# Instructions placed anew in a fused two-layer attention kernel: L0's fours, an attention transfer, odd norms, output weights, a copy and the last store

## The chip, the cores and the metric

The kernel runs on one core of a Trainium2 chip. The metric is the device time of one execution in microseconds (us), the median of several runs. The core has five engines with a queue of instructions each: the tensor engine (PE, with its weight loads shown apart as PEld), the vector engine (DVE), the scalar engine (ACT), GpSimd (POOL) and the sync engine (SP), which here only issues DMAs. POOL and ACT issue DMAs too. Each engine takes its instructions in the order in which they were written; a semaphore makes one wait for another engine.

## The reference

Two layers run one after the other on x and c (`ctx_1024`), both 32 batches of 256 tokens with 256 features in float32.

```python
# L0: 16 heads of 16 features; only batch 0 of the attention is used
q, k, v = x @ Wq.T, c @ Wk.T, c @ Wv.T           # split into heads
att = softmax(q k^T / 4) v
x = x + att[0]                                   # the same 256x256 block for all 32 batches

# L1: one head, a small hidden layer (4 wide), then a second attention
nX = layernorm(c, norm1)                         # keys and values
nF = layernorm(x, norm2)                         # queries
a  = softmax(nF nX^T / 16) nX
h  = gelu(a @ fc1_w.T + fc1_b)                   # 256 -> 4
ca = h @ fc2_w.T + fc2_b                         # 4 -> 256
n  = layernorm(ca, norm3)
s  = softmax(n n^T / 16) n
out = nF + gamma2 * (ca + gamma1 * s)
```

## The kernel before

**Layout.** Of a batch, partition p holds tokens 2p and 2p+1, so a tile is 128 x 2 x 256; the first of the two rows is called even and the second odd. `x_all` keeps all of x in SBUF, in place from the load to the output. c comes in fours of batches (`cq`). The order of instructions is written out by hand (`tc.manual_schedule()`): the order of the Python calls is the order in each engine's queue.

**L0 (the head, to about 35 us).** Only batch 0 is attended. The 16 heads go in four groups of four, j = 0 to 3, called "fours". For each: `head_queries(j)` makes the scores sq with queries as rows (eight products, L445); `head_maxima` takes their row maxima on DVE (L486) into `m_all`; `head_less(j)` transposes these maxima (pm) and returns an addition on DVE that folds them into `qmT` (L498); `head_keys(j)` makes the scores sk with keys as rows and their exponentials on ACT (L507); `head_values(j)` sums the values (ph, L357) and copies them to `col_h`; `head_turned(j)` transposes this (pt_h) and returns the division on DVE (L527, L528) that writes a quarter of `att`. The scores use six PSUM banks in turn; ph, pt_h, pm, pp_v, p_b1f share two banks of the tag "tp", and a tile that takes a bank waits for the last reader of the one before it. Between these stand small preparations: `project_values(1)` (pp_v), `setup_bias` (p_b1f, and `fc1b_all` on DVE), and `stats(n)`, the statistics of c's batch n (two DVE instructions, L211), from which `moments_c` makes the factors of the layernorm on POOL (the power at L227 is the long one), and `even_normed` (POOL) and `odd_normed` (ACT) apply them. `moments_ahead(2)` does its first part on DVE.

**att to x.** x0 to x3 get att by additions on DVE (`add_first`, L828). For the other batches `add_attention(lo, hi)` issues on POOL's queue a DMA that adds att to four batches of x_all (L751): seven transfers of 1 MB.

**L1's first attention.** `first_step(s)` runs for s = 0 to 34, one batch a step, in a software pipeline: in step s the scores of batch s are made (`cross_scores`, L779), their maxima taken on DVE (nm, L789) and their exponentials on ACT (e, L792). In the same step e of batch s-2 is transposed (`cross_turned`, pt_e) and copied by ACT to eTq (L801); x of batch s+1 is transposed (`turn_x`, pt_x) and scaled by ACT into nfT (L761); c of batch s+4 is transposed (`turn_c`, pt_c) and copied by DVE into nxT. `norm_x(n)` applies the layernorm to x: the even row on POOL (L329), the odd row on ACT (L331), up to four steps ahead of use. In every fourth step `moments_both` makes the factors of four batches of x and c on POOL. pt_x and pt_c alternate in the two "tp" banks, so that pt_x takes the bank of the last pt_c, and the other way round. Tables by step, `between` (before the scores) and `beside` (after the step), place the rest: `hide` and `activate` (the Gelu), `third_a` to `third_d` (the third layernorm and its products, w_k on POOL at L1010, t_k on DVE at L1055), `early_scores` and `early_weights` (the first pieces of the second attention), and the output weights: `output_gammas` (two products of 5 x 256 on DVE), `output_bias` (two), and `output_rows` (two, then eight small DMAs on SP that write w_out). In steps 27, 29 and 31 `cross_turned(s-2)` comes after the exponentials.

**L1's second attention.** From about 175 us a written list of words gives the order. "q", "k" and "o" are products, "max", "exp" and "sums" belong to the softmax, "scale" multiplies x by norm2's weight on POOL (L770), "add" adds two batches of output to x_all on DVE (L1214) and stores them with one DMA on SP (L1215).

Of the kernel before, what the change touches and what calls it, by code (L numbers as in the profile page):

```python
# [22 lines left out]
QB = 4  # L23
# [4 lines left out]
def tile_xattn_seq(  # L28
# [33 lines left out]
    nc = tc.nc  # L62
# [261 lines left out]
            )  # L324

    def norm_x(n, even=nc.gpsimd):
        rs, nmr, i = mx_of.pop(n)
        row = x_all[:, n, 0, :]
        even.tensor_scalar(row, row, rs[:, i, :], nmr[:, i, :], ALU.mult, ALU.add)  # L329
        row = x_all[:, n, 1, :]  # L330
        nc.scalar.activation(  # L331
            row, row, AF.Identity, bias=nmr[:, i + 1, :], scale=rs[:, i + 1, :]
        )
# [93 lines left out]
    def project_values(t, copy):  # L427
        pp = bank("tp", f"pp_v{t}")
        for dc in range(NC):
            nc.tensor.matmul(  # L430
                pp[:, t, :],
                c0T[:, dc, t * P : (t + 1) * P],
                wvT[:, dc, :],
                start=(dc == 0),
                stop=(dc == NC - 1),
            )
        copy(v1[:, t, :, 0:DK], pp[:, t, :].rearrange("p (h e) -> p h e", e=DK))
# [39 lines left out]
    def head_queries(j):  # L477

        sq = four_banks(f"sq{j}")
        qk = qT[:, j, :], kT[:, j, :]  # L480
        pair_products((0, *qk, sq[0:2]), (1, *qk, sq[2:4]))
        return sq

    def head_maxima(j, sq, heads):
        for i in heads:
            nc.vector.tensor_reduce(  # L486
                m_all[:, j % 2, :, i, ones_at[j % 2]], sq[i], AX.X, ALU.max, negate=True
            )
# [11 lines left out]
    def head_keys(j):  # L500

        sk = four_banks(f"sk{j}")
        kq = kT[:, j, :], qmT[:, j % 2, :]
        pair_products((0, *kq, sk[0:2]), (1, *kq, sk[2:4]))
        eT_of[j] = wk.tile([P, QB, NC, D], F32, tag="eTq", name=f"eT_h{j}", bufs=2)
        for i in range(QB):
            nc.scalar.activation(eT_of[j][:, i], sk[i], AF.Exp)  # L507
# [68 lines left out]
    def setup_bias():  # L576
        pb = bank("tp", "p_b1f")
        for dc in range(NC):
            nc.tensor.matmul(
                pb[:, 0, 0:FH], ones, b1f[:, dc, :], start=(dc == 0), stop=(dc == NC - 1)  # L580
            )
        nc.vector.tensor_add(fc1b_all, pb[:, 0, 0:FH], fc1b_bc)
# [82 lines left out]
    def stats(*ns):  # L665
        for n in ns:
            stats_c(n)
# [22 lines left out]
    head_less(1)()  # L690
    setup_outer()
    stats(3)
    project_values(1, on_scalar)
    moments_c(0)
    even_normed(0, 1, 2, 3)
    sq = head_queries(2)
    stats(4)
    head_maxima(2, sq, (0, 1))
    head_values(0)
    setup_bias()  # L700
    head_maxima(2, sq, (2, 3))
    head_keys(1)
    odd_normed(0, 1)
    weighted = head_turned(0)
    stats(5)
    head_less(2)()
    weighted()
    sq = head_queries(3)
    stats(6)
    head_maxima(3, sq, range(QB))  # L710
    head_values(1)
    odd_normed(2, 3)
    head_keys(2)
    weighted = head_turned(1)
    stats(7)
    moments_c(1)
    even_normed(4, 5)
    head_less(3)()
    weighted()
    head_keys(3)  # L720
    stats(8, 9, 10)
    head_values(2, by_vector)
    stats(11)
    odd_normed(4)
    head_values(3, on_scalar, True)
    c_ends = moments_ahead(2)
    weighted = head_turned(2), head_turned(3)
    for f in weighted:
# [21 lines left out]
    def add_attention(lo, hi):  # L750
        nc.gpsimd.dma_start(  # L751
            x_all[:, lo:hi],
            att.unsqueeze(1).to_broadcast([P, hi - lo, NC, D]),
            accum_op=ALU.add,
        )
# [38 lines left out]

        return softmax

    def cross_turned(n):
        q, b = n // QB, n % QB
        if b == 0:
            eT_of[q] = wk.tile([P, QB, NC, D], F32, tag="eTq", name=f"eTq_{q}", bufs=2)  # L800
        nc.scalar.copy(eT_of[q][:, b], turned(e_of.pop(n), "et", f"e_{n}"))  # L801

    def values(q):

# [64 lines left out]
    def first_step(s, between=()):  # L869
        q, b = s // QB, s % QB  # L870
        if b == 0 and 2 <= q and q + 4 < NQ:
            load_c(q + 4)
            if q == 2:
                load_x((NQ - 2) * QB, B)
        if s in (2, QB):
            add_attention((s // 2 + 2) * QB, (s // 2 + 3) * QB)
        elif b == 0 and 1 < q < NQ - 3:
            add_attention((q + 3) * QB, (q + 4) * QB)

        late_turn = s in (27, 29, 31)  # L880
        if 0 <= s - 2 < B and not late_turn:
            cross_turned(s - 2)
        if 2 <= s < 2 * QB:
            for n in (2 * s, 2 * s + 1):
                stats_x(n)
            if s < QB:
                ends = first_moments(2 * s, 2 * s + 2)
        if QB <= s and s + 3 * QB < B:
            stats_c(s + 3 * QB)
        if s >= 2 * QB and s + 2 * QB < B:  # L890
            stats_x(s + 2 * QB)
        if b == QB - 1 and 4 <= q + 2 < NQ:
            if q + 3 < NQ:
                moments_both(q + 2)
            else:
                moments_x(q + 2, 0, QB)
        if QB < s < B - 1:
            turn_x(s + 1)
        for n in {9: (12,), 10: (13, 14), 11: (15,)}.get(s, ()):
            norm_x(n)  # L900
        if 3 * QB <= s < B - 2 * QB:
            norm_x(s + QB)
        elif B - 2 * QB < s <= B - QB:
            norm_x(s + QB - 1)
        if s + QB < B and s >= QB:
            turn_c(s + QB, on_scalar if s < QB + 2 else by_vector)
        for n in {7: (13,), 8: (14, 15), 9: (16, 17), 10: (18,)}.get(s, ()):
            norm_c(n)
        if 2 * QB + 2 < s < B - 2 * QB:
            norm_c(s + 2 * QB)  # L910
        for n, at in enumerate(scaled_at):
            if s == at:
                scale_skip(n)
        if 2 * QB <= s < 2 * QB + len(zeroed):
            nc.gpsimd.memset(*zeroed[s - 2 * QB])
        if b == 2 and 1 < q < NQ:
            values_turned(q)
        if b == 1 and 1 < q < NQ:
            values(q)
        if b == 2 and 0 < q <= NQ:  # L920
            cross_values(q - 1)
        if b == 3 and 0 < q <= NQ:
            cross_weighted(q - 1)
        for f, *args in between:
            f(*args)
        if s < B:
            softmax = cross_scores(s)
            if s <= QB:
                turn_x(s + 1)
            if s == 0:  # L930
                turn_c(6, nc.scalar.copy)
            softmax()
        if late_turn:
            cross_turned(s - 2)
        if 1 <= s <= QB:
            stats_c(s + 3 * QB - 1)
        if s == 0:
            first_ends.pop()()
            add_first(3)
            first_ends.append(first_moments(3, QB))  # L940
            odd_normed(7)
        elif s == 1:
            first_ends.pop()()
            odd_normed(8)
            even_normed(8, 9)
        elif s == 2:
            ends()
            turn_c(7)
            load_c(5)
            odd_normed(9)  # L950
            even_normed(10)
        elif s == 3:
            ends()
            values(1)
            even_normed(11)
        elif s == QB:
            values_turned(1)
        if s in (QB, QB + 1):
            odd_normed(s + 6)
        if s == QB:  # L960
            moments_x(2, 0, 2)
        elif s == QB + 1:
            norm_x(2 * QB)
            moments_x(2, 2, QB)
        elif s == QB + 2:
            norm_x(2 * QB + 1)
            moments_c(3)
            norm_x(2 * QB + 2)
            norm_c(3 * QB)
        elif s == QB + 3:  # L970
            norm_x(2 * QB + 3)
        elif s == 2 * QB:
            moments_both(3)
# [179 lines left out]
    def activate(lo):  # L1153
# [1 line left out]

    between = {
        20: [(hide, 0, 4)],
        24: [(output_gammas,)],
        25: [(output_bias,)],
        27: [(output_rows,)],  # L1160
        28: [(turn_t, 0, by_vector)],
        29: [(turn_u, 2, by_vector), (early_weights, 0), (hide, 4, 6)],
        30: [(activate, 4), (third_a, 2), (turn_t, 1, by_vector)],
# [3 lines left out]
        20: [(activate, 0), (third_a, 0)],  # L1167
        21: [(third_b, 0), (third_a, 1)],
        22: [(third_c, 0), (third_b, 1)],
        24: [(third_d, 0)],  # L1170
        25: [(third_c, 1), (turn_u, 0, by_vector)],
        26: [(turn_u, 1, by_vector), (early_scores, 0), (third_d, 1)],
        28: [(early_scores, 1)],
# [37 lines left out]
    def output(p, pieces):  # L1211
# [2 lines left out]
            nc.vector.tensor_add(xs, po, xs)  # L1214
        nc.sync.dma_start(by_tokens(out[2 * p : 2 * p + 2]), x_all[:, 2 * p : 2 * p + 2])  # L1215


    held = {}

# [35 lines left out]
    turn_t6 add8 scale27 sums7 tT6 add7 turn_v5 col7 scale28 o9@s1+k12@s0 vT5 k13@et  # L1255
    add9 exp12 scale29 turn_a7 exp13 o10@s0+o11@s1 scale30 a7 sums6 add10 scale31
    turn_v7 col6 add11 vT7 turn_a6 o15@s0+o14@et a6 turn_v6 add15 vT6 o12@s1 add14
    o13@s0 add12 add13
    """

    def turn_a(g):
# [15 lines left out]
    def pre(lo):  # L1277
# [9 lines left out]
        "max": lambda p: scores_max(p, held.pop(("q", p))),  # L1287
        "exp": lambda p: weights(p, held.pop(("k", p))),
        "add": lambda p: output(p, held.pop(("o", p))),
        "a": lambda g: divide(g, held.pop(("a", g))),  # L1290
        "sums": sums,
        "col": col,
# [69 lines left out]
```

## Time and profile before

| | us |
|---|---|
| median of three runs | 227.26 (227.24 to 228.19) |
| the profiled execution: time | 228.16 |
| its span, first to last instruction | 226.4 |
| PE busy | 208.1 (92% of the span) |
| POOL busy | 175.3 (77%) |
| DVE busy | 169.8 (75%) |
| ACT busy | 146.6 (65%) |
| granted TensorE clock, mean | 0.992 |

The durations in this document come from the one profiled execution, whose time is 0.9 us above the median and whose span leaves 1.8 us around it. A row of the timeline gives start, length, engine, line, operation, output<-input, shapes, the count of equal instructions in the row, and in brackets the idle time before it with the one that ended it. Lengths of instructions that follow each other overlap a little, since an engine starts one before the last has left it: what an instruction costs its queue is the distance between starts.

### The profile page before, as it was taken

What the parts mean: (1) busy time and instruction counts of PE and PEld (TensorE: products, weight loads), DVE (VectorE), ACT (ScalarE), POOL (GpSimd) and SP (SyncE); (2) the same over time, 40 slices, a digit from 0 to 9 for tenths busy, and PEclk for the clock granted to TensorE, in tenths of its full rate; (3) what the DMA queues carried; (4) which work ended last, traced back from release to release, by engine and by line L of the source; (5) the groups of instructions that cost most, each with busy time, mean ns of one, the idle gap of its engine ahead of it and who ended that gap; (6) DMA issues with size and microseconds to landing.
All of it is one profiled execution on the core that took longest, in us unless ns stands there. A gap on an engine that the chain in (4) does not pass through costs nothing.

```text
span 226.4 us, 4951 instructions
## 1 busy us (share of the span) xinstructions
PE 208.1 (92%) x1797; PEld 152.6 (67%) x1797; DVE 169.8 (75%) x406; ACT 146.6 (65%) x301; POOL 175.3 (77%) x276
## 2 busy tenths in 40 slices
PE   7899988898999989999999999998998999999960
PEld 6666547576787859688798697685756566666640
DVE  2787989898988766768767578596546699978791
ACT  2454877698979359576868986448594684545510
POOL 6056588567889999999979989999229888999700
PEclk9999999999999999999999999999999999999996
DMA  6699998998976994082280000000000031542786
GB/s 210 214 310 375 389 386 225 179 263 246 208 145 244 305 195 185 0 147 43 48 142 0 1 3 0 0 3 5 5 1 0 3 126 62 210 164 92 278 308 254
DMA packets 18038, 33.81 MB, mean 149 GB/s; under 512 B 1175, under 2 KB 2142, under 8 KB 18014
## 3 DMA queue, kind: packets, MB, share of 16 engines
q1 hardware_dynamic: 12974, 24.33, 30.1%
q0 software_dynamic: 3696, 7.34, 18.6%
q10 hardware_dynamic: 1344, 1.84, 2.5%
q8 instruction: 14, 0.23, 0.4%
q14 instruction: 10, 0.08, 0.1%
HBM read 17.73 MB, written 8.39 MB: 115 GB/s over the span
## 4 chain that ended last, share of the span: by engine, by line
PE 45%; POOL 22%; DVE 14%; DMA 8%; ACT 5%; issue 3%; DVEq 1%; ACTq 0%; SPq 0%; POOLq 0%
PE sc L779 8%; POOL cq L307 6%; PE o L445 4%; DMA x_all<-att 4%; POOL rs_b L227 4%; PE k L445 4%; DVE st L211 4%; PE pu L357 4%; POOL x_all L329 3%; PE sc L445 2%; PE q L445 2%; DVE nm L789 2%; DMA wk_nat<-in_L_xattn_Wk_dram 2%; DMA fc_nat<-in_L_xattn_fc_w_dram 2%; POOL rs_x L227 2%
## 5 line engine op out<-in xcount | busy, mean ns | idle before, releaser
L779 PE MATMUL sc<-nxT,nfT 128*128 128x256 f32 x256 | 62.4, 386 | 0.7 <-ACT nfT L761 0.7
L779 PEld LDWEIGHTS sc<-nxT,nfT 128*128 128x128 f32 x256 | 45.7, 190 | 12.1 <-issue 5.3
L770 POOL TENSOR_TENSOR x_all<-x_all,w_bc 128x512 f32<-128x512 f32 x32 | 39.8, 1278 | 0.0
L792 ACT ACTIVATE e<-sc,nm 128x256 f32<-128x256 f32 x64 | 26.9, 474 | 19.2 <-DVE nm L789 19.0
L789 DVE TENSOR_REDUCE nm<-sc 128x2 f32<-128x512 f32 x32 | 22.0, 688 | 22.3 <-PE sc L779 10.7
L761 ACT ACTIVATE nfT<-pt_x,bq,wq 128x256 f32<-128x256 f32 x64 | 33.3, 583 | 1.6 <-PE pt_x L202 1.5
L211 DVE BATCH_NORM_STATS2 st<-x_all 128x6 f32<-128x256 f32 x64 | 23.2, 412 | 1.5 <-DMA x_all<-att 1.4
L202 PE MATMUL pt_x<-ident,x_all 128*128 128x128 f32 x132 | 20.4, 276 | 1.5 <-POOL x_all L329 1.3
L202 PE MATMUL pt_c<-ident,cq 128*128 128x128 f32 x132 | 19.7, 276 | 1.9 <-ACT nfT L761 1.4
L1214 DVE TENSOR_TENSOR x_all<-o,x_all 128x1024 f32<-128x1024 f32 (+1 forms) x20 | 19.3, 1005 | 2.9 <-PE o L445 2.4
L202 PE MATMUL pt_e<-ident,e 128*128 128x128 f32 x128 | 19.5, 275 | 1.3 <-ACT eTq L801 0.7
L211 DVE BATCH_NORM_STATS2 st<-cq 128x6 f32<-128x256 f32 x56 | 20.6, 412 | 0.0
L1209 ACT ACTIVATE eT<-k 128x512 f32<-128x512 f32 (+1 forms) x19 | 14.3, 798 | 9.1 <-PE k L445 7.8
L307 POOL TENSOR_SCALAR cq<-cq,rs_b,nmr_b 128x256 f32<-128x256 f32 x32 | 19.4, 679 | 0.0
L202 PEld LDWEIGHTS pt_e<-ident,e 128*128 128x128 f32 x128 | 15.4, 141 | 5.0 <-ACT e L792 1.6
L801 ACT COPY eTq<-pt_e 128x512 f32<-128x512 f32 x32 | 18.4, 588 | 0.3 <-PE pt_e L202 0.3
L202 PEld LDWEIGHTS pt_x<-ident,x_all 128*128 128x128 f32 x132 | 15.2, 141 | 4.6 <-POOL x_all L329 2.4
L202 PEld LDWEIGHTS pt_c<-ident,cq 128*128 128x128 f32 x132 | 15.0, 141 | 3.6 <-ACT nfT L761 2.4
L345 DVE COPY nxT<-pt_c 128x512 f32<-128x512 f32 x23 | 15.6, 677 | 2.4 <-PE pt_c L202 2.4
L331 ACT ACTIVATE x_all<-x_all,nmr_b,rs_b 128x256 f32<-128x256 f32 x16 | 9.8, 619 | 11.0 <-POOL nmr_b L236 11.0
L445 PE MATMUL o<-w_out,vt 32*128 32x256 f32 x128 | 13.3, 400 | 0.6 <-ACT vt L1088 0.5
L445 PE MATMUL k<-tt,ut 32*128 32x256 f32 x112 | 13.6, 397 | 0.0
(222 smaller groups left out, 435.6 us busy)
## 6 DMA issues: line engine op xcount, KB each, us to landing
out_dram<-x_all SPq DMA_DIRECT2D x16, 512.0 KB
x_all<-att POOLq DMA_DIRECT2D x7, 1024.0 KB, 9.8
cq<-in_ctx_dram SPq DMA_DIRECT2D x6, 1024.0 KB
x_all<-in_x_dram SPq DMA_DIRECT2D x4, 1024.0 KB
x_all<-in_x_dram SPq DMA_DIRECT2D x1, 2048.0 KB
x_all<-in_x_dram SPq DMA_DIRECT2D x1, 1792.0 KB
cq<-in_ctx_dram ACTq DMA_DIRECT2D x1, 1024.0 KB
cq<-in_ctx_dram SPq DMA_DIRECT2D x1, 768.0 KB
```

Of the source, the lines that this page charges most:

```text
L202: nc.tensor.transpose(pt[:, dc, t * P : (t + 1) * P], src[:, t, dc * P : (dc + 1) * P], ident)
L211: nc.vector.bn_stats(st[:, t, :], src[:, t, :])
L307: nc.gpsimd.tensor_scalar(row, row, rs[:, i + t, :], nmr[:, i + t, :], ALU.mult, ALU.add)
L345: copy(nxT_of[q][:, b], pt)
L445: nc.tensor.matmul(dst[i][:, t, :], lhs[r : r + SL, t * P : (t + 1) * P], rhs[r : r + SL, :], start=True, stop=True,)
L761: nc.scalar.activation(nfT_of[n][:, dc, :], px[:, dc, :], AF.Identity, bias=bq[:, dc : dc + 1], scale=wq2[:, dc : dc + 1],)
L770: nc.gpsimd.tensor_mul(x_all[:, n], x_all[:, n], w2_bc.unsqueeze(1).to_broadcast([P, NC, D]))
L779: nc.tensor.matmul(sc[:, qt, :], nfT[:, dc, qt * P : (qt + 1) * P], nxT[:, dc, :], start=(dc == 0), stop=(dc == NC - 1),)
L789: nc.vector.tensor_reduce(nm, sc, AX.X, ALU.max, negate=True)
L792: nc.scalar.activation(e[:, qt, :], sc[:, qt, :], AF.Exp, bias=nm[:, qt : qt + 1])
L801: nc.scalar.copy(eT_of[q][:, b], turned(e_of.pop(n), "et", f"e_{n}"))
L1214: nc.vector.tensor_add(xs, po, xs)
```

## The change

No computation is added or left out. Six things are placed anew:

1. In L0 the third four's maxima come at once, followed by the second four's keys; statistics of c's batches 4 to 7 and `setup_bias` stand at other places; the first two divisions come later; `head_values(2)` copies by ACT and not by DVE; the fourth four's values come before the statistics of batch 11.
2. `add_attention(12, 16)` is issued in step 0, behind the even row of x2, and not at the start of step 2.
3. `norm_x` is taken apart. The even rows stay; the odd rows of x12, x14, x16, x17 and x20 (x12 from step 9 to 10, x14 from 10 to 11, x16 from 12 to 13, x20 from 16 to 17) go with the next one.
4. `output_gammas` and `output_bias` go from before the scores of steps 24 and 25 to the end of step 23, `output_rows` from before the scores of step 27 to the end of step 24.
5. In step 31 e29's copy to eTq is DVE's and not ACT's.
6. The last pair of outputs is added and stored batch by batch.

```diff
@@ norm_x @@
     def norm_x(n, even=nc.gpsimd):
-        rs, nmr, i = mx_of.pop(n)
+        even_x(n, even)
+        odd_x(n)
+
+    def even_x(n, even=nc.gpsimd):
+        rs, nmr, i = mx_of[n]
         row = x_all[:, n, 0, :]
         even.tensor_scalar(row, row, rs[:, i, :], nmr[:, i, :], ALU.mult, ALU.add)
+
+    def odd_x(n):
+        rs, nmr, i = mx_of.pop(n)
         row = x_all[:, n, 1, :]
         nc.scalar.activation(
@@ L0 @@
     stats(3)
+    sq = head_queries(2)
+    stats(4)
     project_values(1, on_scalar)
     moments_c(0)
     even_normed(0, 1, 2, 3)
-    sq = head_queries(2)
-    stats(4)
-    head_maxima(2, sq, (0, 1))
+    head_maxima(2, sq, range(QB))
+    head_keys(1)
+    head_less(2)()
     head_values(0)
-    setup_bias()
-    head_maxima(2, sq, (2, 3))
-    head_keys(1)
+    stats(5, 6)
+    sq = head_queries(3)
     odd_normed(0, 1)
     weighted = head_turned(0)
-    stats(5)
-    head_less(2)()
-    weighted()
-    sq = head_queries(3)
-    stats(6)
     head_maxima(3, sq, range(QB))
     head_values(1)
     odd_normed(2, 3)
     head_keys(2)
-    weighted = head_turned(1)
+    setup_bias()
+    head_less(3)()
     stats(7)
     moments_c(1)
     even_normed(4, 5)
-    head_less(3)()
     weighted()
     head_keys(3)
+    weighted = head_turned(1)
+    weighted()
+    head_values(2)
     stats(8, 9, 10)
-    head_values(2, by_vector)
+    head_values(3, on_scalar, True)
     stats(11)
     odd_normed(4)
-    head_values(3, on_scalar, True)
     c_ends = moments_ahead(2)
@@ cross_turned @@
-    def cross_turned(n):
+    def cross_turned(n, copy=nc.scalar.copy):
...
-        nc.scalar.copy(eT_of[q][:, b], turned(e_of.pop(n), "et", f"e_{n}"))
+        copy(eT_of[q][:, b], turned(e_of.pop(n), "et", f"e_{n}"))
@@ first_step @@
-        if s in (2, QB):
-            add_attention((s // 2 + 2) * QB, (s // 2 + 3) * QB)
+        if s == QB:
+            add_attention(QB * QB, (QB + 1) * QB)
...
         for n in {9: (12,), 10: (13, 14), 11: (15,)}.get(s, ()):
-            norm_x(n)
+            even_x(n)
         if 3 * QB <= s < B - 2 * QB:
-            norm_x(s + QB)
-        elif B - 2 * QB < s <= B - QB:
+            even_x(s + QB)
+
+        for n in {10: (12, 13), 11: (14, 15), 12: (), 13: (16, 17), 16: (), 17: (20, 21)}.get(
+            s, (s + QB,) if 3 * QB <= s < B - 2 * QB else ()
+        ):
+            odd_x(n)
+        if B - 2 * QB < s <= B - QB:
             norm_x(s + QB - 1)
...
         if late_turn:
-            cross_turned(s - 2)
+            cross_turned(s - 2, by_vector if s == B - 1 else on_scalar)
...
         if s == 0:
             first_ends.pop()()
+            add_attention(3 * QB, 4 * QB)
             add_first(3)
@@ between, beside @@
         20: [(hide, 0, 4)],
-        24: [(output_gammas,)],
-        25: [(output_bias,)],
-        27: [(output_rows,)],
         28: [(turn_t, 0, by_vector)],
...
         22: [(third_c, 0), (third_b, 1)],
-        24: [(third_d, 0)],
+        23: [(output_gammas,), (output_bias,)],
+        24: [(third_d, 0), (output_rows,)],
         25: [(third_c, 1), (turn_u, 0, by_vector)],
@@ output @@
+    def output_each(p, pieces):
+
+        (_, _, po), = pieces
+        for n in range(2):
+            xs = x_all[:, 2 * p + n]
+            nc.vector.tensor_add(xs, po[:, n], xs)
+            nc.sync.dma_start(by_tokens(out[2 * p + n : 2 * p + n + 1]), x_all[:, 2 * p + n : 2 * p + n + 1])
...
-    o13@s0 add12 add13
+    o13@s0 add12 each13
...
+        "each": lambda p: output_each(p, held.pop(("o", p))),
```

## The prediction

> **What bounds the kernel now.** I read the chain of waits first, then the timeline of each engine at the places the diff touches, then busy time by stage. The page gives the tensor engine 92% of the span, so a place matters only if the tensor engine loses time there, or if a chain of other engines sets when it may go on. The chain of waits between 62 and 130 us (start, length, what) shows such a chain:
>
> ```profile
> 108.77 1.10 POOL cq L307 x2
> ...
> 109.96 9.85 DMA x_all<-att
> ...
> 119.90 0.75 DVE st L211 x2
> ...
> 126.71 0.66 PE pt_c L202 x4
> ```
>
> From 57 us to 115 us GpSimd runs without a gap (its timeline shows no idle there). The last attention transfer stands in that run at 109.96, lands 9.85 later, holds the vector engine's statistics of x28 to 119.90, and through maximum, exponential, Gelu and nfT it reaches a tensor engine that has waited 0.39 at 126.71. So whatever is gained between 57 and 126 counts only if GpSimd's run starts earlier. That start is a vector-engine chain. In the head (timeline of the vector engine; the bracket is the idle time before the row and who ended it):
>
> ```profile
> 20.31 1.29 DVE L486 TENSOR_REDUCE m_all<-sq 128x2 f32<-128x512 f32 x2 [0.97 <-PE sq L445]
> 21.87 0.16 DVE L582 TENSOR_TENSOR fc1b_all<-p_b1f,fc1b_bc 128x4 f32<-128x4 f32 x1 [0.27 <-PE p_b1f L579]
> ...
> 23.14 0.74 DVE L211 BATCH_NORM_STATS2 st<-cq 128x6 f32<-128x256 f32 x2
> 23.88 0.42 DVE L498 TENSOR_TENSOR qmT<-pm,qT 128x256 f32<-128x256 f32 x1
> ...
> 33.74 0.21 DVE L527 RECIPROCAL rd_h<-pt_h 128x8 f32<-128x8 f32 x1 [0.61 <-PE pt_h L375]
> ...
> 34.84 0.69 DVE L828 TENSOR_TENSOR x_all<-x_all,att 128x512 f32<-128x512 f32 x1
> ```
>
> The vector engine has few gaps up to 34.84, where L0 ends, and two more (0.54, 0.51) up to 56.7. After 126.7 the tensor engine is nearly gapless (0.28 at 142.6, 0.87 at 155.05, 0.67 at 174.35). The end is a stream of stores: the DMA engines are full (share 0.98 to 1.06) from 219 to 224.5.
>
> **1. L0's order.** No work is added; col_h2 (0.33 between starts) moves from vector to scalar engine. I walk from qmT of the second four (17.61, unchanged). Spacings from the rows: maximum 0.60, one statistic 0.33, last maximum to qmT 0.65 to 0.73 (two transposes between), score product to first maximum 1.16, p_b1f to fc1b_all 0.65.
> - Statistics of c3, c4 to 19.27; the products sq2 now run before pp_v1, so the four maxima follow at once: 19.27 to 21.69. qmT2 22.41 (1.5 earlier than before), with 0.72 idle, since stats(5), which covered it, now stands behind; c5's and c6's statistics and the next maxima are queued behind that wait.
> - Statistics c5, c6 to 24.07. On the tensor engine pm 22.25, ph0 23.25, sq3: first maximum 24.41 (idle 0.34), last to 26.83. Before: 27.70.
> - But pt_h0, ph1, sk2 and p_b1f fill the tensor engine to 27.37, and pm3 takes p_b1f's bank, so it waits for fc1b_all (27.48; idle 0.65). qmT3 28.24 (idle 0.66), only 0.2 earlier.
> - c7's statistics, att0, a wait for pt_h1 behind sk3 (0.59), att1, then eight statistics (2.63), five moments (0.75): rd_h2 at 34.2, where before it was at 33.74.
> The idle sum goes from 2.2 to 2.96, work falls by 0.33: **L0 ends 0.43 later** (-0.2 to +1.4: below, if the last heads come by the scalar engine's path, whose exponentials are 0.24 earlier; above, if sq3 and sk2 stretch as before, 1.47 and 1.65 us instead of 1.08).
>
> **2. The transfer of x12 to x15** goes past rs of x3, its even row and c8, c9 on GpSimd's queue:
>
> ```profile
> 47.00 0.69 POOL L227 TENSOR_TENSOR rs_x<-ve_x,neg_half 128x2 f32<-128x2 f32 x1 [1.18 <-DVE ve_x L226]
> ...
> 50.13 1.28 POOL L751 DMA_DIRECT2D x_all<-att  x1
> 50.99 1.49 POOL L227 TENSOR_TENSOR rs_x<-ve_x,neg_half 128x4 f32<-128x4 f32 x1
> ```
>
> ```profile
> 52.52 0.16 DVE L236 TENSOR_TENSOR nmr_x<-nmean_x,rs_x 128x4 f32<-128x4 f32 x1 [0.51 <-POOL rs_x L227]
> ```
>
> Its issue holds the queue 0.86 and the power behind it takes 1.49 where its equal at 55.35 takes 1.01. Without it rs starts at 50.75 (ve ends 50.68), ends 51.8, and nmr goes at 52.01: **-0.51**. In the new place the queue idles 1.18, longer than the issue; if rs of x3 also ends 0.48 late it is at 48.2, and nmr wants it at 48.29. If that cover is gone: +0.2. The transfer needs its x, loaded by 36 us (the loads' queue q1 is silent from 38), and joins the accumulate queue behind x8 to x11, which landed at 51.5 and are wanted at 57.1; it shares with c5, wanted at 70.6. Nothing.
>
> **3. Odd norms on the scalar engine** (one activation, 0.60, each; same number):
>
> ```profile
> 81.79 0.60 ACT L331 ACTIVATE x_all<-x_all,nmr_b,rs_b 128x256 f32<-128x256 f32 x1 [5.14 <-POOL nmr_b L236]
> ```
>
> Four such waits sum to 11.0 us, with an exponential behind each. Set a step later they no longer hold it, and the tensor engine's losses at 82.8 and 84.56 (0.52, 0.41, some stretch; four steps of score products take 16.6 and 15.9 there, from 71.70 and 88.31, against 15.11 from 104.21) go: up to 2.3 us. But x15's even row is GpSimd's at 93.2 to 93.7, so at most 1.15 is kept, and the vector engine still stands until the transfer of x28 lands. **Value 0** (-1.1 to 0).
>
> **4. Output weights.** The rows that leave steps 24, 25 and 27, and what they hold:
>
> ```profile
> 151.76 0.95 DVE L654 TENSOR_TENSOR g2r<-g2r,bias 5x256 f32<-5x256 f32 x1
> ...
> 152.97 0.67 DVE L789 TENSOR_REDUCE nm<-sc 128x2 f32<-128x512 f32 x1
> ```
>
> ```profile
> 155.05 1.63 PE L445 MATMUL sc<-ut 32*128 32x256 f32 x16 [0.87 <-ACT eTq L801]
> ```
>
> nm27 could go at 151.76; exponential, eTq and the products at 155.05 follow. They lose 0.87 and a stretch of 0.55 (1.63 against 1.08), so 1.21 of vector time is worth **-1.21**. The rows of 24 and 25 stand before waits for scores and are worth nothing.
> The price is at step 23. Four products come after nm23 (free at 134.46) and before the copy nxT28, and the transposes of x26 (137.08) take that copy's bank. Free they take 4 x 0.41: nxT28 ends 136.8, no loss. But:
>
> ```profile
> 135.35 1.34 POOL L1010 TENSOR_TENSOR w_k<-u_sl,gram_k 128x576 f32<-128x576 f32 x1
> ```
>
> ```profile
> 135.72 1.24 DVE L646 TENSOR_TENSOR g1r<-g1r,g2r 5x256 f32<-5x256 f32 x1
> ...
> 139.58 0.40 DVE L650 TENSOR_TENSOR tail<-tail,g1r 5x256 f32<-5x256 f32 x1
> ```
>
> g1r took 1.24, ending 0.27 after GpSimd's w_k; tail took 0.40 inside GpSimd's power (138.53 to 140.18). The Trainium skill, page SBUF — State Buffer, section Who interferes with whom, speaks against the change here: a vector instruction with two SBUF inputs contends with a GpSimd instruction that reads SBUF, and the later one blocks fully. By the rule the fourth product, dependent on the third, loses to w_k: nxT28 ends 138.3, the tensor engine loses 1.29, and all of the gain is gone (226.8 in all). By the free rows it loses 0 (225.5 in all). The power's row shows that not every GpSimd instruction blocks, and w_k may itself be the loser; then its followers are up to 0.95 late, and x27's even row (140.76, wanted 141.75) costs 0.5. I take +0.5. The two row products after t_k in step 24 lie in the vector engine's slack before nm25 (0.72, and the 0.8 that left); the eight w_out transfers leave SP's queue some 14 us earlier, with only stores behind. **Sum -0.7** (-1.2 to +0.6).
>
> **5. The copy of e29 by the vector engine:**
>
> ```profile
> 174.35 0.66 PE L202 MATMUL pt_e<-ident,e 128*128 128x128 f32 x4 [0.67 <-ACT eTq L801]
> ```
>
> The transposes of e31 wait for e29's bank, whose copy stood behind e31's exponentials. On the vector engine it follows nm31 at 172.9 and ends 173.55; the exponentials end 173.83, so the transposes go at 173.88: **-0.47**. ut3 and the division behind it are 0.6 later; their products start at 177.4 and 178.5. If that cover fails: 0.
>
> **6. The last store** in two halves: one add of 1.13 becomes two of 0.60 between starts, and one issue (0.37) more on SP. The first half is ready 0.5 earlier, the second 0.1 later; the DMA engines have a megabyte before them either way. **0** (-0.3 to +0.1).
>
> **Sum.** +0.43 - 0.51 + 0 - 0.7 - 0.47 + 0 = -1.25. The profiled execution took 228.16 (span 226.4 and 1.8 around it), 0.9 above the median of the runs; against it the sum is 226.9, against the median 227.26 it is **226.0**. A difference of 0.5% (1.14 us) is about what a measurement of this kernel can tell from none.
>
> **Rivals.**
> - Paid back at step 23: w_k blocks the products for its whole length, 1.29 lost for 1.21 won; with 0.43 - 0.51 - 0.47 left the time is 226.8. For it: g1r's row. Against it: tail's.
> - Slower, by the head: if sq3 and sk2 keep their stretched lengths, p_b1f, fc1b_all and pm3 come 1.0 later, L0 ends 1.4 later, and GpSimd's run with it; with step 23 paid back the time is 227.26 + 1.4 - 0.51 + 0.08 - 0.47 = 227.8. It decides from an L0 end more than 1.1 later (1.7 if step 23 costs only 0.5). Against it: those lengths held waits that the new order removes.
> - The odd norms count: transfers landed in 8.6 to 13.8 us; if that of x28 lands in 8.7 instead of 9.85, the vector engine is not held, 1.1 more is kept, and the time is 224.9. Against it: it ran with the DMA engines nearly empty already.
> - The change does what it says; the order of instructions shows it.
>
> **How the numbers follow.** My sum 0.40, step 23 paid back 0.22, head 0.18, odd norms 0.20. My sum is good for +-0.9 and lies just past 0.5%: 0.58 of it faster, 0.37 same, 0.05 slower. Paid back: 0.05, 0.90, 0.05. Head: 0.05, 0.35, 0.60. Odd norms: 0.95, 0.05, 0. Together faster 0.44, same 0.42, slower 0.14. The range reaches from the odd norms' case to just past the head's: 224.8 to 227.9.
>
> **What would show it.** Right: x0's add with att at 35.2 to 35.4; no wait of 0.5 at nmr of x4; no 5.14 wait at 82, but x28's statistics still waiting for the transfer, longer than 0.94; nm27 right after n_all; e31's transposes without 0.67. Wrong: the add before 34.8 or after 36; the tensor engine at 126.7 - 1 or earlier; over a microsecond of waiting at x26's transposes.

## The result: 0.2% faster, a third of what was forecast

| | kernel before | changed kernel |
|---|---|---|
| median of 15 runs each | 227.49 (226.87 to 228.29) | 227.08 (226.29 to 227.62) |
| the profiled execution: time | 228.16 | 226.61 |
| its span | 226.4 | 224.8 |
| PE / DVE / ACT / POOL busy | 208.1 / 169.8 / 146.6 / 175.3 | 207.0 / 169.9 / 146.9 / 174.2 |

The ratio is 0.9981, with a 95% interval of 0.9967 to 0.9994: 0.43 us are won, between 0.14 and 0.75. The forecast was 1.25. The two profiled executions lie 1.55 apart, almost four times as much as the medians, so a part of what their rows show belongs to the one execution and not to the kernel. Which part, the experiments tell.

First the chain of waits of the changed kernel (start, length, what), the four lines that answer to those of before:

```profile
108.40 1.09 POOL cq L307 x2
...
109.58 9.34 DMA x_all<-att
...
119.02 0.75 DVE st L211 x2
...
126.06 0.66 PE pt_c L202 x4
```

The last attention transfer is still in the chain, and the tensor engine still waits at 126.06 (0.69); how much of that the transfer makes, the late statistics tell below. The head, in the timeline of the vector engine:

```profile
24.07 2.49 DVE L493 TENSOR_REDUCE m_all<-sq 128x2 f32<-128x512 f32 x4 [0.27 <-PE sq L452]
27.12 0.16 DVE L589 TENSOR_TENSOR fc1b_all<-p_b1f,fc1b_bc 128x4 f32<-128x4 f32 x1 [0.56 <-PE p_b1f L586]
27.87 0.42 DVE L505 TENSOR_TENSOR qmT<-pm,qT 128x256 f32<-128x256 f32 x1 [0.59 <-ACT eT_h L514]
...
29.90 0.21 DVE L534 RECIPROCAL rd_h<-pt_h 128x8 f32<-128x8 f32 x1 [0.51 <-PE pt_h L382]
...
35.00 0.69 DVE L833 TENSOR_TENSOR x_all<-x_all,att 128x512 f32<-128x512 f32 x1
```

The first rows of this execution began 0.31 earlier than before's (the second four's addition into qmT at 17.30, not 17.61, where both kernels are alike). In the 14 profiles of this study that row lies between 16.84 and 18.06, whatever the kernel. So below, **inside** means from that row to the end of the span: 208.76 in the first profile of before, 207.53 in the changed kernel. Counted from there x0's addition with att comes at 17.70, and in before at 17.23: L0 ends 0.47 later.

GpSimd's queue, where the transfer of x12 to x15 now stands:

```profile
46.00 1.31 POOL L756 DMA_DIRECT2D x_all<-att  x1
47.23 0.84 POOL L227 TENSOR_TENSOR rs_x<-ve_x,neg_half 128x2 f32<-128x2 f32 x1
...
50.98 1.01 POOL L227 TENSOR_TENSOR rs_x<-ve_x,neg_half 128x4 f32<-128x4 f32 x1 [0.57 <-DVE ve_x L226]
```

The power of x4 takes 1.01 and not 1.49, and GpSimd now waits 0.57 for its input. The vector engine's 0.51 in front of nmr_x is gone.

The output weights at the end of step 23 (vector engine; then GpSimd; then the tensor engine):

```profile
133.82 0.40 DVE L653 TENSOR_TENSOR g1r<-g1r,g2r 5x256 f32<-5x256 f32 x1
134.26 0.41 DVE L654 TENSOR_TENSOR g2r<-g2r,m 5x256 f32<-5x256 f32 x1
134.60 0.55 DVE L657 TENSOR_TENSOR tail<-tail,g1r 5x256 f32<-5x256 f32 x1
135.18 1.44 DVE L658 TENSOR_TENSOR g2r<-g2r,tail 5x256 f32<-5x256 f32 x1
136.55 0.67 DVE L352 COPY nxT<-pt_c 128x512 f32<-128x512 f32 x1
```

```profile
134.95 1.40 POOL L1021 TENSOR_TENSOR w_k<-u_sl,gram_k 128x576 f32<-128x576 f32 x1
```

```profile
137.37 0.63 PE L202 MATMUL pt_x<-ident,x_all 128*128 128x128 f32 x4 [0.78 <-POOL sq_x L224]
```

The fourth product was given out 0.23 after GpSimd's w_k had begun, and ended 0.27 after it. The copy nxT28 stands behind it and ends at 137.22; the transposes of x26 take that copy's bank and had been ready 0.78 earlier. (The bracket names sq_x, since that was over at 137.34. But x26 does not wait for it: with the weights put back, below, the same transposes go at 136.33, before their sq_x at 136.90. It is the bank.)

### The profile page after: what moved, and what is told of

Read it like the earlier page. It is cut to its first block, busy times and chain, and to the rows that moved or that the text cites. A ratio compares the mean times of both kernels' runs of the same rounds, so it can differ in the third digit from the quotient of the medians.

```text
span 224.8 us, 4960 instructions
## 1 busy us (share of the span) xinstructions
PE 207.0 (92%) x1797; PEld 152.7 (68%) x1797; DVE 169.9 (76%) x407; ACT 146.9 (65%) x301; POOL 174.2 (77%) x276
## 4 chain that ended last, share of the span: by engine, by line
PE 38%; POOL 26%; DVE 13%; ACT 5%; DMA 4%; issue 3%; DVEq 0%; POOLq 0%; ACTq 0%
PE sc L784 7%; POOL cq L307 6%; PE o L452 4%; DMA x_all<-att 4%; POOL rs_b L227 4%; PE k L452 4%; DVE st L211 4%; PE pu L364 4%; PE q L452 2%; POOL x_all L333 2%; PE sc L452 2%; POOL rs_c L227 2%; DVE nm L794 2%; PE pv L364 2%; POOL x_all L756 2%
## 5 line engine op out<-in xcount | busy, mean ns | idle before, releaser
L1223 DVE TENSOR_TENSOR x_all<-o,x_all 128x1024 f32<-128x1024 f32 (+1 forms) x19 | 18.1, 994 | 2.9 <-PE o L452 2.4
L806 ACT COPY eTq<-pt_e 128x512 f32<-128x512 f32 x31 | 17.9, 584 | 0.2 <-PE pt_e L202 0.2
L1205 DVE TENSOR_REDUCE t_sl<-q 128x4 f32<-128x1024 f32 (+1 forms) x12 | 12.3, 1041 | 0.3 <-PE q L452 0.2
```

## The experiments

All times are set against the kernel before run beside them on the same chip; its median moved from chip to chip between 227.4 and 228.0, so the ratios compare better than the medians. "Landing" is the time from the issue of the last attention transfer to its landing, "to step 24" from the row above to the scores of batch 24.

| run | median | ratio (95%) | inside | landing | to step 24 |
|---|---|---|---|---|---|
| before, first profile | | | 208.76 | 9.85 | 117.31 |
| before, second profile | | | 208.17 | 8.55 | 116.77 |
| changed | 227.08 | 0.9981 (0.9967-0.9994) | 207.53 | 9.34 | 116.97 |
| L0's order back | 226.33 | 0.9948 (0.9928-0.9968) | 207.32 | 9.42 | 116.73 |
| odd norms back | 227.20 | 0.9982 (0.9968-0.9997) | 207.60 | 8.44 | 117.09 |
| transfer back | 227.23 | 0.9995 (0.9982-1.0008) | 207.84 | 9.27 | 117.32 |
| weights back | 227.04 | 0.9979 (0.9967-0.9992) | 207.81 | 9.39 | 117.10 |
| e29's copy back | 227.67 | 0.9986 (0.9967-1.0004) | 208.31 | 9.37 | 117.21 |
| last store back | 227.15 | 0.9969 (0.9954-0.9985) | 207.82 | 9.28 | 117.19 |
| head back, rows in 26 | 225.28 | 0.9889 (0.9862-0.9916) | 206.08 | 9.40 | 116.55 |
| late statistics | 225.51 | 0.9896 (0.9869-0.9924) | 206.26 | 9.25 | 115.64 |
| late statistics, odd norms back | 226.84 | 0.9955 (0.9942-0.9969) | 207.38 | 8.58 | 116.79 |
| both of the above gains | 223.79 | 0.9834 (0.9801-0.9867) | 204.80 | 9.35 | 115.26 |
| before with late statistics | 227.34 | 0.9990 (0.9975-1.0004) | 208.17 | 8.48 | 116.75 |

Four of these kernels do the same up to the scores of batch 24: the changed one and those with the weights, e29's copy or the last store put back. Their last column has 116.97, 117.10, 117.21 and 117.19, a scatter of 0.24 with a mean of 117.12, and the changed kernel's own profile is the lowest. So a difference of less than some 0.25 between two single profiles up to step 24 shows nothing.

### The kernel before, profiled again

No edit.

> The kernel before once more, unchanged, for a second profile of it: the first profile counts 208.76 us from the first add into qmT of the second four (17.61) to the end, the changed kernel's 207.53, a difference of 1.23, while the medians differ by 0.4. Theory (the forecast's terms were measured against an execution of before that was unlucky by some 0.7 within the program): this profile counts 208.0 to 208.3, and the rows show where. Rival (the first profile was ordinary): 208.6 to 208.9 again, and the difference of the medians is lost ahead of 17 us.

Inside it counts 208.17, 0.59 less, and the rows show where. Two of them, vector engine and tensor engine:

```profile
118.46 0.74 DVE L211 BATCH_NORM_STATS2 st<-x_all 128x6 f32<-128x256 f32 x2
```

```profile
125.83 0.66 PE L202 MATMUL pt_c<-ident,cq 128*128 128x128 f32 x4
```

Neither has a bracket. The transfer landed 8.55 after its issue (at 118.00), before the vector engine came to the statistics of x28, and the tensor engine did not wait at 126. Up to step 21 the two executions agree within about 0.1; at step 24 they are 0.54 apart. The wait with which the prediction opens stands in one of the two profiles of this kernel and not in the other. Against this profile the changed kernel is 0.64 ahead, which lies in the interval of the medians (0.14 to 0.75); against the first it was 1.23. Why the transfer landed late in the first is told with the hardware, at the end.

### L0's order of before

```diff
-    sq = head_queries(2)
-    stats(4)
     project_values(1, on_scalar)
     moments_c(0)
     even_normed(0, 1, 2, 3)
-    head_maxima(2, sq, range(QB))
-    head_keys(1)
-    head_less(2)()
+    sq = head_queries(2)
+    stats(4)
+    head_maxima(2, sq, (0, 1))
...
```

> The changed kernel with L0's order of before; all else as changed. Theory (the new L0 order costs 0.4 to 0.5 us): x0's add with att about 0.45 earlier relative to the first rows, the factors of x4 as much earlier, and the time 226.6 against 227.08 for the changed kernel, that is 0.85 under the kernel before. Rival (the head is absorbed on the way to 126 us, as the chain there is closed by the last attention transfer's landing): x0's add earlier, but the last attention issue and the time as in the changed kernel, 227.1.

x0's addition came at 17.24 (changed: 17.70), the factors of x4 at 34.52 (35.03). So the new order costs 0.46 at L0's end and 0.51 in front of the transfers' chain. At the end 0.2 of it is left against the one profile of the changed kernel, and 0.39 at step 24 against the mean of the four; the ratio says 0.75 (0.9948 against 0.9981), with an uncertainty of some 0.5. The cost is real; its size at the end lies between 0.2 and 0.75.

### The odd norms of before

```diff
         for n in {9: (12,), 10: (13, 14), 11: (15,)}.get(s, ()):
-            even_x(n)
+            norm_x(n)
         if 3 * QB <= s < B - 2 * QB:
-            even_x(s + QB)
-
-        for n in {10: (12, 13), 11: (14, 15), 12: (), ...
-            odd_x(n)
-        if B - 2 * QB < s <= B - QB:
+            norm_x(s + QB)
+        elif B - 2 * QB < s <= B - QB:
             norm_x(s + QB - 1)
```

> The changed kernel with the odd norms back in the steps of before; all else as changed. Theory (the odd norms are worth nothing at the end): the scalar engine's waits for GpSimd's factors come back (5.14 and three smaller ones), the scores of batch 16 come about 2 us later than in the changed kernel, those of batch 22 within 0.2 of it, and the time is 227.1, within 0.2 of the changed kernel. Rival (the odd norms carry the small gain): 0.5 to 1.1 slower than the changed kernel, 227.6 to 228.2.

The timeline of the scalar engine here, and then that of the changed kernel at the same place:

```profile
81.21 0.60 ACT L338 ACTIVATE x_all<-x_all,nmr_b,rs_b 128x256 f32<-128x256 f32 x1 [5.14 <-POOL nmr_b L236]
```

```profile
81.51 1.09 ACT L338 ACTIVATE x_all<-x_all,nmr_b,rs_b 128x256 f32<-128x256 f32 x2 [0.87 <-POOL nmr_b L236]
```

The wait of 5.14 is back, and the scores of batch 16 come 1.96 later, counted from inside's first row. At step 24 it is 0.12, at the end 0.07, and the ratios are the same (0.9982, 0.9981). The odd norms win two microseconds by step 16 and keep none.

### The transfer of before

```diff
-        if s == QB:
-            add_attention(QB * QB, (QB + 1) * QB)
+        if s in (2, QB):
+            add_attention((s // 2 + 2) * QB, (s // 2 + 3) * QB)
...
-            add_attention(3 * QB, 4 * QB)
```

> The changed kernel with the transfer of x12 to x15 issued at the start of step 2 again; all else as changed. Theory (the place in step 0 is worth 0.4): the power behind the issue takes 1.49 again and not 1.01, the factors of x4 and all issues of GpSimd to 110 us come 0.4 later, and the time is 227.5. Rival (absorbed later): the factors of x4 later, but the time 227.1.

The power behind the issue, and nmr_x behind that:

```profile
51.35 1.49 POOL L227 TENSOR_TENSOR rs_x<-ve_x,neg_half 128x4 f32<-128x4 f32 x1
```

```profile
52.88 0.16 DVE L236 TENSOR_TENSOR nmr_x<-nmean_x,rs_x 128x4 f32<-128x4 f32 x1 [0.50 <-POOL rs_x L227]
```

The factors of x4 come 0.40 later, all of GpSimd's issues with them, and the end 0.31 (by the ratios 0.32). So the place in step 0 is worth 0.40 at the factors. What of it reaches the end is not shown: at step 24 it is 0.20 over the mean of the four, within their scatter, and the ratio is uncertain by 0.4.

### The output weights of before

```diff
     between = {
...
+        24: [(output_gammas,)],
+        25: [(output_bias,)],
+        27: [(output_rows,)],
...
     beside = {
...
-        23: [(output_gammas,), (output_bias,)],
-        24: [(third_d, 0), (output_rows,)],
+        24: [(third_d, 0)],
```

> The changed kernel with the output weights back in front of the scores of steps 24, 25 and 27; all else as changed. Theory (the place in step 23 costs 0.97 and the rows' gain in step 27 is 1.2): the wait of 0.78 at the transposes of x26 goes, the wait of 0.87 before the products at 155 comes back, and the time is 0.2 over the changed kernel, 227.3. Rival (the forecast's price of 0.5 for step 23): 0.7 over it, 227.8.

Vector engine, then tensor engine:

```profile
134.97 1.23 DVE L653 TENSOR_TENSOR g1r<-g1r,g2r 5x256 f32<-5x256 f32 x1
```

```profile
136.33 0.60 PE L202 MATMUL pt_x<-ident,x_all 128*128 128x128 f32 x4
...
154.26 1.63 PE L452 MATMUL sc<-ut 32*128 32x256 f32 x16 [0.83 <-ACT eTq L806]
```

The blocked product is now g1r, but nothing that the tensor engine wants stands behind it: its transposes of x26 do not wait. From the scores of 24 to those of 25 it takes 4.13, and 5.10 with the weights in step 23. From the scores of 28 to those of 29 it takes 8.12 and 6.96. So step 23 costs 0.97 and step 27 gives 1.16. In every profile of this study these distances are, for the same place of the weights, the same within 0.03. The gain of this part is 0.2; the end is 0.28 later here, and the ratios are alike.

### e29's copy on the scalar engine, and the last store as one

```diff
-            cross_turned(s - 2, by_vector if s == B - 1 else on_scalar)
+            cross_turned(s - 2)
```

> The changed kernel with e29's copy on the scalar engine again. Theory (the copy by the vector engine is worth 0.5 at the end): the transposes of e31 wait again, 2.1 after nm31 and not 1.43, and the time is 0.5 over the changed kernel, 227.6. Rival (the later ut3 and the division take it back): 0, 227.1.

The transposes of e31, first of the changed kernel and then of this one:

```profile
172.81 0.73 PE L202 MATMUL pt_e<-ident,e 128*128 128x128 f32 x4
```

```profile
173.99 0.66 PE L202 MATMUL pt_e<-ident,e 128*128 128x128 f32 x4 [0.67 <-ACT eTq L806]
```

They come 2.09 after nm31 instead of 1.43. The changed kernel keeps 0.57 of these 0.66 up to the last add (47.22 against 47.13 from here). Inside is 0.78 longer, 0.24 of it already at step 24, where this edit has not acted yet: such is the difference between two executions. The ratios can't tell a gain of 0.5 from none (0.9986, up to 1.0004, against 0.9981); it rests on the rows.

```diff
-    o13@s0 add12 each13
+    o13@s0 add12 add13
```

> The changed kernel with the last two batches added and stored as one. Theory (the halves let the last store begin earlier): 4.9 us from the end of the last add to the end and not 4.75, the last add ending 0.1 earlier, and the time within 0.15 of the changed kernel, 227.1. Rival (the last megabyte waits for its start): 0.4 over it, 227.5.

From the end of the last add to the end it takes 4.93, and 4.74 to 4.79 with the halves; the add ends up to 0.07 earlier. So the halves give about 0.1, which the ratio (0.9969) can't show.

### Late statistics: where the odd norms' gain went

```diff
         if s >= 2 * QB and s + 2 * QB < B:
-            stats_x(s + 2 * QB)
+            for n in {16: (), 17: (24,), 18: (25, 26), 20: (), 21: (28,), 22: (29, 30)}.get(s, (s + 2 * QB,)):
+                stats_x(n)
```

> The changed kernel with the statistics of x24 and x28 one step later (and those of x25, x26, x29 and x30 moved up against them), so that the vector engine doesn't stand for the last two attention transfers. Theory (what the odd norms win by step 16 is lost only in these waits): the vector engine's wait of 1.68 and the tensor engine's of 0.40, 0.48 and 0.69 between 104 and 127 go, the scores of batch 24 come 1.1 to 1.5 earlier, and the time is 1.1 to 1.5 under the changed kernel, 225.8. Rival (GpSimd's factors for x24 to x27, which come at 120, bind next): at most 0.4 under it, 226.7 or more.

The changed kernel ran into the transfer (vector engine, then tensor engine):

```profile
119.02 0.75 DVE L211 BATCH_NORM_STATS2 st<-x_all 128x6 f32<-128x256 f32 x2 [1.68 <-DMA x_all<-att]
119.69 0.67 DVE L352 COPY nxT<-pt_c 128x512 f32<-128x512 f32 x1
```

```profile
120.51 0.63 PE L202 MATMUL pt_x<-ident,x_all 128*128 128x128 f32 x4 [0.48 <-DVE nxT L352]
```

Its vector engine stood 1.68 for x28's statistics, and behind these stand the copy nxT24, a bank, and the transposes of x22. For those of x24 it had stood 0.94, at 103.36. With the statistics a step later (vector engine, then tensor engine):

```profile
117.86 0.69 DVE L352 COPY nxT<-pt_c 128x512 f32<-128x512 f32 x1 [0.56 <-PE pt_c L202]
...
120.27 0.74 DVE L211 BATCH_NORM_STATS2 st<-x_all 128x6 f32<-128x256 f32 x2
```

```profile
119.82 0.60 PE L202 MATMUL pt_x<-ident,x_all 128*128 128x128 f32 x4
...
125.23 0.66 PE L202 MATMUL pt_c<-ident,cq 128*128 128x128 f32 x4 [0.57 <-ACT nfT L766]
```

No wait for the transfer is left on either engine. The scores of 24 come 1.33 earlier, the end 1.27; the ratio falls from 0.9981 to 0.9896, that is 1.9 us with an uncertainty of 0.7. The edit acts at two transfers: 0.53 of the 1.33 is there at the scores of batch 20, before x28's statistics have moved, so it is the transfer of x24 to x27 that had taken this, and the last one the other 0.8. One part of the expectation missed: 0.57 remains at 125.23, so most of that wait belongs to the Gelu and nfT on the scalar engine and not to the transfer.

> The same late statistics, with the odd norms back in the steps of before. Theory (the odd norms are worth their 1.5 to 2 us once the last transfer no longer takes them): 1.1 to 2.0 slower than with the late statistics alone, 227.0 to 227.8. Rival (they are worth nothing in any case, since another chain sets 126 us): within 0.3 of it.

With the odd norms of before on top, inside is 1.12 longer, and the median 1.33. So the odd norms are worth 1.1 to 1.3, and nothing as long as the vector engine stands for the two transfers.

> The kernel before with nothing changed but the late statistics of x24 and x28. Theory (before loses to the last attention transfer only in those executions in which it lands late, 0.5 in the first profile and nothing in the second): no wait for the transfer, and 0.1 to 0.4 under the kernel before, 227.2; the changed kernel with late statistics then stands 1.7 below it, the sum of all its parts with the odd norms at 1.1. Rival (the transfer costs before as much as the changed kernel): 1.1 under it, 226.4.

The same edit in the kernel before is worth nothing that can be measured (0.9990, up to 1.0004; inside 208.17, equal to before's second profile). Before does not wait for the last transfer unless it lands late. The changed kernel, further ahead, waited in every profile: in all seven with the new odd norms and the statistics in their old place the vector engine stood 1.54 to 1.81 for it, and the scores of batch 24 came 15.33 to 15.41 after its landing. So there it is the landing that sets step 24.

### The version that the experiments point to

```diff
     between = {
...
+        24: [(output_gammas,)],
+        25: [(output_bias,)],
+        26: [(output_rows,)],
...
     beside = {
...
-        23: [(output_gammas,), (output_bias,)],
-        24: [(third_d, 0), (output_rows,)],
+        24: [(third_d, 0)],
```

with L0's order of before.

> The changed kernel with L0's order of before, the gammas and the bias in front of the scores of steps 24 and 25 as before, and the row products in front of the scores of step 26, where the vector engine waits 1.54 for them; transfer, odd norms, e29's copy and the last store as changed. Theory (the head costs 0.2 to 0.45, step 23 costs 0.97, and the rows' gain of 1.2 stays, since two products of 0.41 fit into the gap): no wait at the transposes of x26 nor at the products of 155, and 1.2 to 1.4 under the changed kernel, 225.8. Rival (the rows in front of step 26 hold its maximum): 0.4 to 0.8 worse than that, 226.5.

Both prices are gone and the rows' gain stays: 1.45 under the changed kernel inside, ratio 0.9889. With the late statistics besides:

> Both at once: L0's order of before and the row products in front of step 26, and the late statistics of x24 and x28; transfer, odd norms, e29's copy and the last store as changed. Theory (the losses lie at different places, so their removal adds): 1.1 to 1.3 under either of the two alone, 224.2. Rival (what the earlier head or step 23 gives back is what the late statistics already gave): 225.2, as the better of the two.

```profile
143.33 0.40 DVE L661 TENSOR_TENSOR g2r<-g2r,bias 5x256 f32<-5x256 f32 x1
143.66 0.41 DVE L662 TENSOR_TENSOR g1r<-g1r,k 5x256 f32<-5x256 f32 x1
144.95 0.69 DVE L796 TENSOR_REDUCE nm<-sc 128x2 f32<-128x512 f32 x1 [0.88 <-PE sc L786]
```

```profile
135.49 0.60 PE L202 MATMUL pt_x<-ident,x_all 128*128 128x128 f32 x4
...
152.51 1.36 PE L452 MATMUL sc<-ut 32*128 32x256 f32 x16
```

The two row products fit into the vector engine's gap in front of nm26 and leave 0.88 of it. The losses add: 204.80 inside, 2.73 under the changed kernel; the median is 223.79, and the ratio 0.9834 (0.9801 to 0.9867), 1.7% faster than before.

## Why the prediction was wrong, step by step

The forecast had the sign and most of the mechanisms, and the size three times too large. Two of its terms failed: the price of step 23, which was mis-sized, and the first three steps together, because the landing that bounds them, read in one profile, was taken as fixed. What was measured, counted against the second profile of before, where the transfer had not landed late: +0.20 up to step 24, +0.97 at step 23's price, -1.17 at step 27, -0.66 at e31, +0.15 from there to the last add, -0.12 at the store. That is -0.63. With the mean of the four profiles the first item is +0.35 and the sum -0.48, near the 0.43 of the medians.

- **L0's order** (+0.43 forecast): right. +0.47 at L0's end, and the rows of the walk within 0.1: qmT2 4.77 after the first row (forecast 4.80), fc1b_all 9.82 (9.87), qmT3 10.57 (10.63).
- **The transfer of x12 to x15** (-0.51): -0.40 at the factors. The wait that it removed was 0.51 long, and a fifth of that did not reach them.
- **The odd norms** (0): right in the number, and the bound "at most 1.15 is kept" stands against 1.12 to 1.33 with late statistics; whether x15's even row is what sets it was not tested. That the vector engine would still stand for x28's transfer was right too. But that the transfer was the bound already in before was read off one execution. It is the odd norms themselves that bring the engines to it: the vector engine came to x28's statistics at 117.3 here and at 118.46 in the second profile of before, while the transfer is issued at the same time, 92.28 after the first row against 92.18 and 92.35 (L0's later end and the transfer's new place about cancel there).
- **The first three steps together** (-0.08): a step that failed. They bring +0.20 to +0.35 at step 24 (-0.34 only against the first profile of before, with its late landing). The forecast took the 9.85 of that one profile for the kernel's own, before and after. The second profile has 8.55, and with the new odd norms it is 9.25 to 9.42, for a reason that stands at the end. In all the landing is 0.9 later after the first row than in the second profile (101.6 against 100.7), and the scores of batch 24 follow it. The rival "the odd norms count" had asked for a landing in 8.7. By the 15.4 between landing and scores, a landing after 8.55 would have brought step 24 to 116.2 (an estimate), 0.6 ahead of before. That rival missed on how the odd norms and the landing hang together: the change that wins the time also delays the landing.
- **The output weights** (-0.7): the step that failed most. The gain of step 27 was right (1.21, measured 1.17). The price of step 23 was taken as 0.5, between 0 by the free rows and 1.29 by the rule that the later of two contending instructions blocks fully; it is 0.97. The Trainium skill's page SBUF — State Buffer, section Who interferes with whom, was right on this pair: the product given out during w_k ended 0.27 after it, as g1r had in before. The third product ended 0.27 after GpSimd's u_sl in the same way (134.60 to 135.15; u_sl from 134.27 to 134.87), and in before g2r with the bias took 0.95 instead of 0.40 and ended 0.27 after GpSimd's scaling of x (L770). The power at L227, also an instruction with two inputs by its row, did not block (tail's 0.40): here the measurement differs from the section, which makes no such exception. So tail's row was no evidence for w_k. The price stayed below the rule's 1.29 because only the last of the four products met w_k from behind. So nxT28 ended 2.96 after the first score product of batch 24 (137.22 - 134.26), where the forecast by the rule had 3.39 (138.3 - 134.91).
- **e29's copy** (-0.47): -0.66 at the transposes, 0.5 to 0.57 of it kept. **The last store** (0): about -0.1.

So of the missing 0.6, 0.5 is step 23's price and 0.3 the first three steps (+0.20 where the sum had -0.08), less 0.15 from the copy and the store. The rival "paid back at step 23" came nearest, with 226.8 (0.46 won, 0.43 measured), but partly by luck: it had the weights at +0.08, and they gave 0.20; its first three steps had -0.08, and they cost 0.20 to 0.35. Of the difference between the two profiled executions the rest did not repeat: 0.31 before the first row and 0.54 at the late landing.

## What to carry to other kernels

Before a wait that a single profile shows is made the pillar of a forecast, ask whether it could have been a transfer that landed late: a second profile of the unchanged kernel shows it. A gain ahead of a fixed landing is worth what the queue behind that landing lets through; moving the instructions that wait (the statistics behind two transfers, a step later) turned a gain of nothing into 1.1 to 1.3 us. And filler work goes into a gap of its engine that ends in a wait for something else, not in front of the copy that frees a bank which the tensor engine wants next: the same four products cost 0.97 in step 23 and nothing in front of steps 24 and 25, and the two rows cost 1.16 in front of step 27 and nothing in front of step 26.

## What the runs showed of the hardware

- The last attention transfer, 1 MB, landed 9.25 to 9.42 after its issue in all nine profiles with the new odd norms, and in 8.44 to 8.58 in four of the five with the old ones (9.85 in the fifth). The sizes and the queue are the same. The packet records of the traces show what differs: a load of the core's own instructions, one packet of 16 KB on another queue (q8, kind "instruction"), which takes 0.9 to 1.1 us. For the last two attention transfers of the 14 profiles:

  | the load begins, after the issue | transfers | last packet ends | landing |
  |---|---|---|---|
  | 1.2 to 1.7 (around its first packets) | 9 | 7.64 to 7.89 | 7.94 to 8.19 |
  | 3.3 to 7.0 (in the midst) | 14 | 8.90 to 9.12 | 9.21 to 9.43 |
  | 7.88 to 8.11 (nearly all over) | 4 | 7.91 to 8.13 | 8.44 to 8.58 |
  | 7.82 (first profile of before) | 1 | 8.78 | 9.85 |

  In the second row the last 7 to 10 packets end one by one, after all others are over, as if one of the 16 DMA engines had been held up by the load; the trace does not name a packet's engine. With the new odd norms the load comes about a microsecond earlier (98.2 to 99.6 after the first row, not 100.2 to 100.5) and falls into the last transfer. In the first profile of before it began when one packet, of 4 bytes, was still to start, and that packet went only at 8.76; in the second the same packet went at 7.99, just ahead of the load. That makes 0.8 of the 1.3 between these two landings; the rest, after the last packet, is open. No run moved the load by itself.
- A vector product of 5 x 256 with two SBUF inputs took 0.40 alone, inside GpSimd's power too, and 1.23 to 1.45 when given out while GpSimd's 128 x 576 product ran, ending 0.27 to 0.28 after it, in all 14 profiles.
- Distances inside the program repeat closely from one execution to another: within 0.03 from step 24 to 25 and from 28 to 29 for the same place of the weights, within 0.15 over the 47 us from e31 to the last add of the kernels with e29's copy on the vector engine. What differs more is when the first rows start (1.2 us between the extremes), when that one transfer lands, and with it step 24 (0.24 among four kernels that are alike up to there).
